# Two of four tiles' membership tests in an experts' routing: from VectorE alone to ScalarE and VectorE

## The chip, the cores and the metric

The kernel runs on one core of a Trainium2 chip. The metric is device time in microseconds (us), the median of several executions. A profiled execution of the kernel gives the trace that the numbers below come from.

## What is computed

Four layers run over an input of 4 batches of 1024 positions with 256 features each: a state space layer, a feed-forward layer, a linear attention layer and the same feed-forward layer again. The change touches the feed-forward layer, which adds an MLP and a product-key mixture of 512 tiny experts:

```
routing = einsum("tnd,tdk->tnk", (h @ W_q).reshape(2, n, 64), keys)   # two scores of 64 keys each
sx, sy = top 8 of each;  all_scores = sx[:, :, None] + sy[:, None, :]  # 64 pairs
scores, pk = top_k(all_scores, 8);  indices = 64 * ix + iy             # 8 experts of 512
ew = silu(x . down_embed[indices]) * softmax(scores)
out = mlp(x) + sum over the 8 of ew * up_embed[indices]
```

Keys of the first kind that can give an expert number below 512 are only the first 8 of 64; a larger number is taken as 511, the last expert.

## The kernel before

The 4096 positions are eight groups of 512, and a group is four tiles of 128 positions (the partitions). The kernel never gathers rows of the experts. For each position it makes a dense table `tb` of 512 weights, almost all of them zero, transposes it on TensorE (`st`), multiplies it into the dense activations `wt` of all experts, and sends that through `up_emb`.

`route` makes the table of one group. Its steps follow each other through small tiles: `r` holds the scores (copied from PSUM by ScalarE), `v` the top 8 values (MAX8 on VectorE), `d` exponentials, `code` a rank code of each of 64 second keys, and `most` a threshold for each of 8 first keys. `entries(m)` fills `tb` for tile `m` with 8 ScalarE activations of 64 elements. The last three operations, on VectorE, compare every code to every threshold (`eq`, 4 tiles x 8 x 64 = 2048 elements), multiply `tb` by this mask of 0 and 1, and add `last` to the last expert's column.

`route` is a Python generator, cut into steps by `yield`. It is used in two places.

In the **experts stage** (`experts`, line label L46 in the trace since a helper records every operation) all engines' queues stand in an order written by hand. A loop takes eight steps `k` per group. In each step it advances `apply` (the table's use for this group, with `emb` products on TensorE and `silu` on ScalarE), then `routes[g]`, then, at k = 5, 6 and 7, `routes[g + 1]` (scores, copy to `r`, top 8 to `v`), and at the end `beside`, which puts in parts of the state space layer's last groups and of their MLP (tiles `gate`, `tanh`, `up`, `av`, `down`, `xw`). The tiles of `route` have one buffer each here. The PSUM banks of `emb`, `gate`, `up`, `down` and others are three, taken in turn. At k = 0 of the next group the transposes `st` of tiles 0 and 1 read `tb`; those of tiles 2 and 3 wait until VectorE has multiplied the first two into `wt`.

In the **last FFN** (`ffn`) a scheduler orders each engine's queue. `route(0)` stands before the first group; `route(g + 1)` stands between `chosen(g)`, which uses the table of g, and `raise_x(g)`, a long run of TensorE products into the output. Each group has eight pairs of products `gate` and `up` into four PSUM banks; ScalarE takes the silu of the first into `s` (L1509), VectorE multiplies it by the second (`act`, L1511).

Of the kernel before, what the change touches and what calls it, by code (L numbers as in the profile page):

```python
# [13 lines left out]
AF = mybir.ActivationFunctionType  # L14
ALU = mybir.AluOpType
# [4 lines left out]
P = 128  # L20
# [4 lines left out]
NG = NT // G  # L25
# [3 lines left out]
NEXP, NKEY, TOPK, INTER = 512, 64, 8, 1024  # L29
# [21 lines left out]
class Net:  # L51
# [1064 lines left out]
    def route(self, nc, w, g, hT, pools, got, ps=None):  # L1116
# [8 lines left out]
        dve = nc.vector  # L1125
# [33 lines left out]
        def eights(name):  # L1159
            return sm.tile([P, M4, TOPK], F32, tag=name, name=name)  # L1160
# [28 lines left out]
        sht = [P, M4, TOPK, NKEY]  # L1189
        tb = tables.tile([P, M4, NEXP], F32, tag="tb", name="tb")  # L1190
        tbv = tb.rearrange("p m (i j) -> p m i j", i=TOPK)
# [20 lines left out]
        code = sm.tile([P, M4, NKEY], F32, tag="code", name="code")  # L1212
# [11 lines left out]
        for i in range(M4):  # L1224
# [5 lines left out]
        first, rank = r[:, 0:M4, 0:TOPK], eights("rank")  # L1230
# [14 lines left out]
        most, last8 = eights("most"), eights("last8")  # L1245
# [15 lines left out]
        eqv = eq.rearrange("p m j b -> p m (j b)").rearrange(  # L1261
            "p m (i j) -> p m i j", i=TOPK
        )
        dve.tensor_tensor(
            eqv, code.unsqueeze(2).to_broadcast(sht),
            most.unsqueeze(3).to_broadcast(sht), ALU.is_ge,
        )
        yield
        dve.tensor_tensor(tbv, tbv, eqv, ALU.mult)
        dve.tensor_tensor(tb[:, :, NEXP - 1], tb[:, :, NEXP - 1], last, ALU.add)  # L1270
        got.append(tb)

# [39 lines left out]
    def experts(self, w, xpool, xs, hs, rest):  # L1312


        tc, nc, ends, mlps, bank = self.tc, rest.engines, rest.ends, rest.mlps, rest.bank
        with ExitStack() as ctx:
# [16 lines left out]
            asks, hT, routes, tables = dict(rest.first_h), {}, {}, {}  # L1333
# [4 lines left out]
            def load(into, g):  # L1338
                while g == NG - 1 and ends.next_cost():
                    ends.stage()  # L1340
                tag = "hT" if into is hT else f"ask{g // half}"
                into[g] = two.tile([P, KD, G], F32, tag=tag, name=tag)
                nc.sync.dma_start(out=into[g], in_=hs[g])
# [7 lines left out]
            def begin(g):  # L1351
                tables[g] = []
                ps = None if g else rest.route0
                routes[g] = self.route(nc, w, g, asks, (one, one, one, rp), tables[g], ps)
                next(routes[g])
# [75 lines left out]
            def beside(cost):  # L1431
                left[0] = min(left[0] + 3.5, 6.0) - cost
                for q in (ends, mlps):
                    c = q.next_cost()
                    if c is not None and c[0] <= left[0]:
                        q.stage()
                        left[0] -= c[0]
# [7 lines left out]
            for step in range(8 * NG + 6):  # L1445
                g, k = step // 8, step % 8
                if k == 0 and g < NG:
                    while g not in rest.stored:
                        ends.stage()
                        mlps.stage()  # L1450
                    self.x[g] = xpool.tile([P, TG, D], F32, tag=f"x{g}", name=f"x{g}")
                    nc.sync.dma_start(out=self.x[g], in_=xs[g])
                if k == 2 and g < NG:
                    applied.append(apply(g))
                for a in list(applied):
                    if next(a, self) is self:
                        applied.remove(a)
                if g < NG:
                    next(routes[g], None)
                if g + 1 < NG:  # L1460
                    if k == 5:
                        begin(g + 1)
                    if k > 5:
                        next(routes[g + 1])

                    if k == 5 and g % 2 == 0 and g + 2 < NG:
                        load(asks, (g + 2) // 2)
                        load(asks, (g + 2) // 2 + half)
                    if k == 6:
                        load(hT, g + 1)  # L1470
                beside(COST[k])

    def ffn(self, w, out):
        nc, tc = self.nc, self.tc
        with ExitStack() as ctx:
# [18 lines left out]
            def route(g):  # L1494
# [3 lines left out]
                return got[0]  # L1498

            table = route(0)  # L1500
            for g in range(NG):
                h = hT[g]
                act = []
                for c in range(IC):
                    cs = slice(c * P, (c + 1) * P)
                    pg = self.product(mm, [(w["gate_w"][:, k, cs], h[:, k, :]) for k in range(KD)])
                    pu = self.product(mm, [(w["up_w"][:, k, cs], h[:, k, :]) for k in range(KD)])
                    s = two.tile([P, G], F32, tag="s", name="s")
                    nc.scalar.activation(s, pg, AF.Silu)  # L1509
                    a = acts.tile([P, G], F32, tag="act", name="act")  # L1510
                    nc.vector.tensor_tensor(a, s, pu, ALU.mult)  # L1511
                    act.append(a)
                wt = self.chosen(two, stp, mm, w, h, table)
                if g + 1 < NG:
                    table = route(g + 1)
                self.raise_x(op, g, w, wt, act)
                self.store(out, g)
# [71 lines left out]
```

## Time and profile before

| what | us |
|---|---|
| median of 3 runs | 2068.34 (2068.19 to 2068.84) |
| the profiled execution's own time | 2070.76 |
| its span, first to last instruction | 2069.0 |
| VectorE busy with `eq<-code,most`, 16 times | 36.6 |
| VectorE busy with `tb<-tb,eq`, 16 times | 36.6 |
| experts stage, from the first table to the last | about 1119 to 1357 of the span |
| last FFN | about 1588 to 2069 of the span |

The span is the profiled time without what lies around it. A row of busy time adds up the instructions of one form; it says how long they ran, not that the kernel would be shorter by as much without them.

### The profile page before, as it was taken

The page shows a single profiled execution, that of the slowest core. Times are in us where ns is not written, and L with a number is a line of the kernel's source. Part 1 is how long each engine was busy: PE and PEld are TensorE (multiplying, and loading weights), DVE is VectorE, ACT ScalarE, POOL GpSimd, SP SyncE. Part 2 cuts the span into 40 slices and gives each one's busy share as a digit, 9 for nine tenths or more (in the row PEclk, how much of TensorE's full clock was granted, in tenths as well). Part 3 has the DMA queues.
Part 4 walks back from the last instruction along what each step waited for, and adds up shares of the span by engine and source line. Part 5 has one row for each costly group of instructions (what it writes and reads, how often), then busy time and mean ns, then how long its engine had stood idle before and what let it go on. Part 6 is the DMA issues. An engine that isn't in the chain of part 4 may idle for free.

```text
span 2069.0 us, 22487 instructions
## 1 busy us (share of the span) xinstructions
PE 1806.8 (87%) x7402; PEld 1156.1 (56%) x7402; DVE 1643.7 (79%) x2845; ACT 1068.9 (52%) x2041; POOL 897.1 (43%) x607
## 2 busy tenths in 40 slices
PE   6777689888789898898868899889997999999999
PEld 2445445546456464564644656656765666556665
DVE  5799999999999999999999999954548644445551
ACT  3866667756777677677354454513333332333331
POOL 2978878888788887787751000011110000000000
PEclk9777899999999999999979999999998999999999
DMA  4111122221222212212123032120000000000000
GB/s 128 41 37 46 46 68 66 76 68 47 80 76 68 72 49 78 65 53 75 54 79 114 14 105 72 31 87 1 1 1 1 0 11 11 10 11 10 11 11 10
DMA packets 79926, 97.45 MB, mean 47 GB/s; under 512 B 7361, under 2 KB 53313, under 8 KB 79809
## 3 DMA queue, kind: packets, MB, share of 16 engines
q1 hardware_dynamic: 73232, 89.35, 14.3%
q10 hardware_dynamic: 6576, 6.67, 1.0%
q8 instruction: 58, 0.95, 0.2%
q14 instruction: 60, 0.48, 0.1%
HBM read 83.15 MB, written 12.85 MB: 46 GB/s over the span
## 4 chain that ended last, share of the span: by engine, by line
PE 44%; DVE 38%; issue 9%; ACT 7%; POOL 1%; DMA 0%; DVEq 0%; SPq 0%; ACTq 0%; POOLq 0%
PE ps L105 23%; DVE h L46 12%; DVE acc L46 10%; PE hT L46 2%; ACT a L46 2%; PE up L46 2%; PE dt L46 2%; PE gate L46 2%; DVE eq L46 1%; PE bc L46 1%; PE o L46 1%; PE out L46 1%; ACT xc L46 1%; PE xin L46 1%; PE tr L96 1%
## 5 line engine op out<-in xcount | busy, mean ns | idle before, releaser
L46 POOL TENSOR_TENSOR u<-dx,bt 128x1024 f32<-128x1024 f32 x255 | 602.6, 2364 | 199.2 <-DVE h L46 134.6
L46 PE MATMUL hT<-ident,h 128*128 128x128 f32 x2048 | 322.8, 299 | 147.4 <-DVE acc L46 145.7
L46 ACT ACTIVATE a<-delta,a_neg 128x512 f32<-128x512 f32 x512 | 342.4, 688 | 198.3 <-DVE h L46 197.1
L46 PEld LDWEIGHTS hT<-ident,h 128*128 128x128 f32 x2048 | 252.0, 152 | 291.1 <-DVE acc L46 251.4
L46 DVE SCALAR_TENSOR_TENSOR acc<-hT,cT,acc 128x512 f32<-128x512 f32 x512 | 354.9, 734 | 15.6 <-PE hT L46 15.2
L46 DVE TENSOR_TENSOR_SCAN h<-a,state,u 128x512 f32<-128x512 f32 x256 | 316.2, 1276 | 2.9 <-ACT a L46 1.6
L46 DVE TENSOR_TENSOR_SCAN h<-a,u 128x512 f32<-128x512 f32 x256 | 302.2, 1222 | 15.1 <-ACT a L46 15.0
L1511 DVE TENSOR_TENSOR act<-s,ps 128x512 f32<-128x512 f32 x64 | 44.0, 688 | 151.4 <-PE ps L105 151.3
L85 POOL TENSOR_TENSOR ri<-ri,mhalf 128x4 f32<-128x4 f32 x16 | 16.1, 1012 | 314.1 <-DVE ri L84 314.0
L46 PE MATMUL gate<-hT,gate_w 128*128 128x512 f32 x256 | 125.9, 615 | 8.8 <-ACT acc L46 8.8
L1509 ACT ACTIVATE s<-ps 128x512 f32<-128x512 f32 x64 | 38.1, 597 | 167.4 <-PE ps L105 164.6
L46 PE MATMUL up<-hT,up_w 128*128 128x512 f32 x256 | 121.9, 599 | 2.9 <-DVE xw L46 2.9
L105 PE MATMUL ps<-hT,w_gate_w 128*128 128x512 f32 x256 | 122.1, 600 | 2.5 <-DVE act L1511 2.5
L46 POOL TENSOR_TENSOR xc<-xc,tap 128x512 f32<-128x512 f32 x84 | 111.4, 1326 | 23.6 <-ACT tap L46 23.5
L46 PE MATMUL down<-w_down_w,av 128*128 128x256 f32 x512 | 119.7, 382 | 1.0 <-DVE xw L46 1.0
L105 PE MATMUL ps<-hT,w_up_w 128*128 128x512 f32 x256 | 120.4, 592 | 0.0
L105 PE MATMUL ps<-w_down_w,act 128*128 128x256 f32 x512 | 116.8, 380 | 3.0 <-DVE x L1308 3.0
L105 PEld LDWEIGHTS ps<-w_down_w,act 128*128 128x128 f32 x512 | 96.0, 190 | 21.6 <-DVE x L1308 8.8
L46 PEld LDWEIGHTS down<-w_down_w,av 128*128 128x128 f32 x512 | 96.1, 192 | 21.2 <-issue 8.6
L46 ACT ACT_TABLE_LOAD x63 | 80.8, 1283 | 29.5 <-DVE d L46 19.4
L1195 ACT ACTIVATE tb<-d,ex 128x64 f32<-128x64 f32 x256 | 62.0, 334 | 53.2 <-DVE ex L1185 53.2
L46 PE MATMUL out<-w_out_wT,y 128*128 128x256 f32 x256 | 70.1, 423 | 18.5 <-DVE y L46 18.3
(253 smaller groups left out, 3080.0 us busy)
## 6 DMA issues: line engine op xcount, KB each, us to landing
bt<-bcd SPq DMA_DIRECT2D x127, 256.0 KB, 3.3
gate_w<-in_gate_w SPq DMA_DIRECT2D x64, 128.0 KB, 2.5
up_w<-in_up_w SPq DMA_DIRECT2D x64, 128.0 KB, 2.2
in_wT<-in_in_wT SPq DMA_DIRECT2D x8, 512.0 KB, 3.8
hs<-hT SPq DMA_DIRECT2D x8, 512.0 KB, 3.0
xs<-xw SPq DMA_DIRECT2D x8, 512.0 KB, 2.7
hT<-hs SPq DMA_DIRECT2D x8, 512.0 KB, 4.3
x<-xs SPq DMA_DIRECT2D x8, 512.0 KB, 4.4
```

What stands on the lines that cost most here:

```text
L46: return self.tc.keep_in_program_order(f(*args, **kw))
L85: nc.gpsimd.tensor_tensor(ri, ri, self.mhalf.to_broadcast([P, TG]), ALU.pow)
L96: self.nc.tensor.transpose(ps[:, t * P : (t + 1) * P], src[:, t, k * P : (k + 1) * P], self.ident)
L105: self.nc.tensor.matmul(ps, lhsT=lhsT, rhs=rhs, start=i == 0, stop=i == len(pairs) - 1)
L1195: nc.scalar.activation(tbv[:, m, i, :], d[:, M4 + m, 0:NKEY], AF.Copy, scale=ex[:, m, i : i + 1],)
L1509: nc.scalar.activation(s, pg, AF.Silu)
L1511: nc.vector.tensor_tensor(a, s, pu, ALU.mult)
```

## The change

For tiles 2 and 3, ScalarE now makes the difference `most - code` (Identity with scale -1 and the threshold as a bias per partition), 8 activations of 64 elements for each tile, and VectorE takes "difference <= 0" and the multiplication by `tb` in one operation with three operands. For tiles 0 and 1 VectorE compares and multiplies as before, over 1024 elements instead of 2048. The generator has one more `yield`, before the fused operation, and in the experts stage step k = 7 advances `routes[g]` once more, after `routes[g + 1]`: the top-8 search of the next group stands before the fused operation.

```diff
+        first, others, shh = slice(0, 2), slice(2, 4), [P, 2, TOPK, NKEY]
+        for m in (2, 3):
+            for i in range(TOPK):
+                nc.scalar.activation(
+                    eqv[:, m, i, :], code[:, m, :], AF.Identity, scale=-1.0,
+                    bias=most[:, m, i : i + 1],
+                )
         dve.tensor_tensor(
-            eqv, code.unsqueeze(2).to_broadcast(sht),
-            most.unsqueeze(3).to_broadcast(sht), ALU.is_ge,
+            eqv[:, first], code[:, first].unsqueeze(2).to_broadcast(shh),
+            most[:, first].unsqueeze(3).to_broadcast(shh), ALU.is_ge,
         )
         yield
-        dve.tensor_tensor(tbv, tbv, eqv, ALU.mult)
+        dve.tensor_tensor(tbv[:, first], tbv[:, first], eqv[:, first], ALU.mult)
+        yield
+        dve.scalar_tensor_tensor(
+            tbv[:, others], eqv[:, others], 0.0, tbv[:, others], ALU.is_le, ALU.mult
+        )
         dve.tensor_tensor(tb[:, :, NEXP - 1], tb[:, :, NEXP - 1], last, ALU.add)
...
                     if k > 5:
                         next(routes[g + 1])
+                if k == 7 and g < NG:
+                    next(routes[g], None)
+                if g + 1 < NG:
 
                     if k == 5 and g % 2 == 0 and g + 2 < NG:
```

## The prediction

> **What bounds the kernel now.** I read the page first, then busy time by stage, then the waits of the stage, then the order of time around the changed lines, since only there can one see which wait ends last.
>
> ```profile
> PE 1806.8 (87%) x7402; PEld 1156.1 (56%) x7402; DVE 1643.7 (79%) x2845; ACT 1068.9 (52%) x2041; POOL 897.1 (43%) x607
> PE   6777689888789898898868899889997999999999
> DVE  5799999999999999999999999954548644445551
> ACT  3866667756777677677354454513333332333331
> ```
>
> The routing runs twice: in slices 22 to 26 (first experts stage) and from slice 31 on (last FFN). In the first VectorE is at 9; in the second TensorE is, and VectorE is half idle. Busy time by stage says it in us (columns: stretch, length, PE, PEld, DVE, ACT, POOL, clock, DMA share, GB/s):
>
> ```profile
> 1119.00:1357.00 238.00, 212.82 (x838) 143.77 (x837) 223.37 (x560) 116.24 (x331) 7.57 (x11) 0.94 0.20 65
> 1588.00:2069.00 481.00, 471.06 (x1645) 292.53 (x1643) 235.60 (x562) 149.44 (x384) 0.00 (x0) 0.99 0.03 9
> ```
>
> VectorE is busy 94% of the experts stage; in the last FFN it is 49%, and TensorE 98%. Who TensorE waits for in the experts stage (us in all, times, longest):
>
> ```profile
> PE st L46 <- DVE wt L46: 14.4, 6, 3.1
> PE st L46 <- DVE tb L46: 9.7, 3, 4.6
> ```
>
> Once a group TensorE stops for VectorE and then runs on almost without a gap until the next such stop. So a delay of VectorE moves everything behind it. In the last FFN the same delay costs nothing unless TensorE waits.
>
> **The change, instruction by instruction.** The groups by form (count | busy us, mean ns | idle before):
>
> ```profile
> L46 DVE TENSOR_TENSOR eq<-code,most 128x2048 f32<-128x2048 f32 x8 | 18.3, 2285 | 0.1
> L46 DVE TENSOR_TENSOR tb<-tb,eq 128x2048 f32<-128x2048 f32 x8 | 18.3, 2287 | 0.4
> L46 DVE SCALAR_TENSOR_TENSOR av<-up,av 128x512 f32<-128x512 f32 x12 | 8.2, 681 | 0.0
> L46 ACT ACTIVATE tb<-d,ex 128x64 f32<-128x64 f32 x256 | 63.0, 336 | 36.8 <-DVE ex L46 36.8
> ```
>
> VectorE loses two passes over 2048 elements (2.29 us each) for each of 16 routings, and gets three over 1024. No pass of 1024 is in the trace. Between the 512 (0.69, the tensor-tensor d<-r,v; 0.68 for the three-operand form above) and the 2048 the slope is 1.04 ns an element, so 1.22 us each, 3.67 instead of 4.58: 0.92 us saved a routing, 14.7 us in all, of which only the 7.3 of the experts stage lie on its path. Bounds for the new three-operand pass: 1.20 to 1.25 from the two 512 rows.
>
> ScalarE gets 16 activations of 64 elements a routing. Nearest row: tb<-d,ex, the same shape with one pointer operand (there scale, here bias). The experts stage in order of time, second routing (start, us, engine, line, operation; the brackets give idle time and who ended it):
>
> ```profile
> 1165.34 0.59 ACT L46 COPY r<-route 128x512 f32<-128x512 f32 x1 [1.19 <-PE route L46]
> ...
> 1166.19 0.42 DVE L46 TENSOR_REDUCE most<-pw 128x32 f32<-128x256 f32 x1
> 1166.65 2.29 DVE L46 TENSOR_TENSOR eq<-code,most 128x2048 f32<-128x2048 f32 x1
> ...
> 1169.19 2.29 DVE L46 TENSOR_TENSOR tb<-tb,eq 128x2048 f32<-128x2048 f32 x1
> ...
> 1171.51 0.17 DVE L46 TENSOR_TENSOR tb<-tb,last 128x4 f32<-128x4 f32 x1
> 1171.59 1.10 DVE L46 MAX8 v<-r 128x8 f32<-128x64 f32 x8
> ...
> 1187.18 3.92 ACT L46 ACTIVATE tb<-d,ex 128x64 f32<-128x64 f32 x16
> ```
>
> Sixteen such activations take 3.92 us (0.239 from start to start). Here a rule of the Trainium skill weighs against the change: "VectorE: DVE Perf Modes", section on the TRN2 errata, holds that the SBUF latency of VectorE and ScalarE is exposed between instructions, so many small tiles pay it each time, and wants 512 elements or more. Taken at its word, 16 times 0.336 is 5.4 us. The row shows overlap, 3.92, and I use that; the rule's figure is the upper end, 1.45 us more for each of nine places below, +13.
>
> **Where it lands: the experts stage.** The built order puts the sixteen activations on ScalarE after silu(1) and ahead of r<-route, the next group's scores. In the rows above r is copied at 1165.34, before "most" is ready at 1166.61. Now r waits behind the sixteen: they start 0.12 us after "most" (the delay of tb behind ex at 1304.62), r starts 3.82 later and takes 0.59. On VectorE the eight MAX8 of the next group now stand between the half multiply and the new fused pass, and they need r. Call the end of "most" M: MAX8 starts at M+4.56, the fused pass 1.02 later (eight starts, 0.127 apart), the small add of "last" 1.25 after that, the next instruction 0.08 later: M+6.91. That includes the fused pass itself, so VectorE idles about 2 us and then does what it did before. Against the time of that next instruction before:
>
> Routing 1: M 1132.62, 1139.53 against 1139.47, +0.06 (two av passes used to sit there and now fill the wait). Routing 2: M 1166.61, 1173.52 against 1172.61, +0.91. Routing 3: M 1199.06, 1205.97 against 1204.92, +1.05. Routing 5: M 1261.74, +0.65. Routing 6: M 1291.24, +0.85. Routing 7: M 1321.59, +0.73 (against 1327.77).
>
> Routing 4 (M 1230.90) is worse, because work of the MLP stands in between:
>
> ```profile
> 1231.41 2.28 DVE L46 TENSOR_TENSOR eq<-code,most 128x2048 f32<-128x2048 f32 x1
> ...
> 1232.10 0.60 ACT L46 ACTIVATE tanh<-gate 128x512 f32<-128x512 f32 x1 [1.19 <-PE gate L46]
> ...
> 1233.62 0.68 DVE L46 SCALAR_TENSOR_TENSOR av<-tanh,gate 128x512 f32<-128x512 f32 x1
> ```
>
> That tanh comes after r in ScalarE's order, so it ends at M+5.02 = 1235.95 instead of 1232.70; VectorE, done with its half compare at 1232.6, stands at av until then. Then av 0.60, half multiply 1.14, MAX8 1.02, fused and last 1.33: 1240.05 against 1237.63, +2.4. TensorE's emb(3) also waits for this av to free a PSUM bank, but it is back before the wt multiply, which VectorE reaches 2.4 us late anyway.
>
> Routing 8 has no next group: fused pass at 1353.19 after the sixteenth activation, last ends 1354.61; the fourth transpose of tile 0 needs it and goes at 1354.75 instead of 1354.37, +0.4.
>
> Sum 7.1 us. It passes on: behind each routing TensorE's second pair of transposes waits for VectorE's wt. silu(2) and silu(3) also slip by 2 to 4 us behind the sixteen; they free PSUM banks, and TensorE loses up to 1 us for them, inside the 1.1 to 3.1 us that it waits for wt. The extra generator step at k=7 issues no instruction of its own and moves no DMA; POOL and SP keep their order.
>
> **Where it lands: the last FFN.** For routings 2 to 8 the sixteen run between tb and the first silu of the next pair while TensorE does the up and down products; in the routing at 1765 they end at 1771.2, with the table load s ends at 1773.0, and VectorE needs it at 1773.05. Cover is 0.05 us for VectorE and over 3 for TensorE, whose bank is wanted at 1776.22. Cost 0. The saved VectorE time is worth nothing there. Routing 1 has no previous group's down products to hide behind:
>
> ```profile
> 1605.49 1.06 ACT L1509 ACTIVATE s<-ps 128x512 f32<-128x512 f32 x2
> ...
> 1606.15 1.95 PE L105 MATMUL ps<-hT,w_gate_w 128*128 128x512 f32 x4
> ```
>
> The gate matmul at 1606.15 takes the bank that the first s frees. Now s starts at 1605.49+3.82 = 1609.3 and ends 1609.9, so TensorE starts at 1610.0, 3.85 late. Six transposes of tb move up into this gap by the new order and give back 0.8: +3.1.
>
> **Sum**: 7.1 + 3.1 = +10.2 us. The profiled execution took 2070.76 us (span 2069.0 and 1.8 around it), the median of the runs is 2068.34; +10.2 makes 2081.0 for the first and 2078.5 for the median.
>
> **Rivals.** Faster: a bias pointer costs ScalarE nothing, and the sixteen run as pointer-free ones would. "ScalarE: Activation LUTs", section "What ACT_TABLE_LOAD costs", states 93 ns for each pointer operand; without it the start-to-start time would be about 0.146 by estimate, and r would be 1.4 us earlier. The waits then fall under the saving in all routings but the fourth: -4 in the experts stage, +1.7 in the FFN, in all about -2; the sign turns where the sixteen take under 2.8 us (1.1 us off nine places). To pass -4.1 (0.2%) the FFN loss must vanish too, and VectorE's 7.3 come through: 2061. Against it: delta<-z with a bias pointer alone takes 687 ns where a plain copy of its size takes 586. Chance 0.05.
>
> Absorbed: half the delay of VectorE disappears in places where it waits for TensorE anyway (x<-o, 6.9 us in the stage). +3, 2071. Against it: those matmuls follow the late transposes. Chance 0.08.
>
> Much slower: no overlap among the sixteen (+13), or a bank freed late by silu(2) stops TensorE outside its idle time, some 1 us in each routing. 2086 to 2092. Chance 0.10.
>
> That the change does not do what it says is excluded by the built order, where all sixteen stand in each of 16 routings.
>
> **Numbers.** The forecast keeps 0.77. Range 2071 to 2086: from the absorbed case to where the much slower one begins. A measurement of this kernel tells about 0.2% (4.1 us) from no change. Faster 0.05, same 0.08, slower 0.87.
>
> **What would show it.** Right: three DVE rows of about 1.22 us; sixteen eq<-code,most on ACT in about 3.9 us; DVE v<-r waiting for ACT r, about 2 us in six of the routings; DVE av waiting for ACT tanh once for over 3 us; TensorE 3 us idle near 1606 of the old time; no change in routings 2 to 8 of the last FFN. Wrong: MAX8 without a wait, activations at 0.15 or 0.33 us, the experts stage (238.0 us before) not longer by 5 to 9 us, or the last FFN by more than 5.

## The result, and the profile after

The changed kernel takes 2079.26 us (median of 5 runs, 2078.35 to 2080.61), the kernel before on the same chip 2068.19 (2067.20 to 2068.84): ratio 1.0056, 95% interval 1.0041 to 1.0070. That is 11.1 us slower; 10.2 were predicted. The profiled execution of the changed kernel took 2078.35 us (span 2076.6).

The page's first line and three rows of slices:

```profile
PE 1807.6 (87%) x7402; PEld 1154.6 (56%) x7402; DVE 1627.9 (78%) x2861; ACT 1128.6 (54%) x2297; POOL 896.4 (43%) x607
...
PE   6767779888789897898877989889997999999999
...
DVE  5899999999999999999999889945548544445551
ACT  3866667766677666776454556523333433434441
```

VectorE has 15.8 us less to do than before (1643.7) and ScalarE 59.7 more (1068.9), yet the kernel is longer. Busy time by stage (stretch, length, PE, PEld, DVE, ACT, POOL, clock, DMA share, GB/s) and the groups of the new instructions:

```profile
1119.00:1357.00 238.00, 207.78 (x828) 139.53 (x828) 212.05 (x564) 142.20 (x451) 7.56 (x11) 0.96 0.20 65
...
1588.00:2076.00 488.00, 475.92 (x1656) 295.10 (x1654) 228.59 (x576) 181.51 (x513) 0.00 (x0) 0.99 0.03 9
```

```profile
L46 ACT ACTIVATE eq<-code,most 128x64 f32<-128x64 f32 x128 | 31.4, 334 | 17.6 <-DVE most L46 17.6
...
L46 DVE TENSOR_TENSOR eq<-code,most 128x1024 f32<-128x1024 f32 x8 | 9.8, 1220 | 0.1
L46 DVE TENSOR_TENSOR tb<-tb,eq 128x1024 f32<-128x1024 f32 x8 | 9.7, 1218 | 0.3
L46 DVE SCALAR_TENSOR_TENSOR tb<-eq,tb 128x1024 f32<-128x1024 f32 x8 | 9.7, 1209 | 1.4 <-ACT eq L46 1.4
```

In the 238 us around the experts stage VectorE falls from 223.37 to 212.05 us of busy time. That is more than the change saves there, since beside the longer stage less of its surroundings fits into the stretch. Between the same two places of the program (M, the end of routing 1's last reduction into `most`, and the end of the eighth addition of `last`) VectorE is busy for 208.8 us before and 200.9 after, and idle for 12.6 and 24.8: 7.9 us of work saved, 12.2 us of idle time added. What the engines wait for is in the waits of the stage (total, times, longest):

```profile
PE st L46 <- DVE wt L46: 15.5, 7, 3.3
PE st L46 <- DVE tb L46: 10.9, 5, 3.4
DVE v L46 <- ACT r L46: 9.3, 6, 1.9
DVE x L46 <- PE o L46: 5.4, 5, 2.4
DVE av L46 <- ACT tanh L46: 3.7, 3, 3.2
```

The third and the last row are new in this size: v<-r did not wait before, and av<-tanh waited 0.4 us. Routing 2 in order of time (start, us, engine, line, operation) shows the cause:

```profile
1163.19 1.23 DVE L46 TENSOR_TENSOR eq<-code,most 128x1024 f32<-128x1024 f32 x1
...
1163.19 3.93 ACT L46 ACTIVATE eq<-code,most 128x64 f32<-128x64 f32 x16 [2.49 <-DVE most L46]
...
1167.03 0.56 ACT L46 COPY r<-route 128x512 f32<-128x512 f32 x1
...
1167.62 1.11 DVE L46 MAX8 v<-r 128x8 f32<-128x64 f32 x8 [1.74 <-ACT r L46]
1168.65 1.21 DVE L46 SCALAR_TENSOR_TENSOR tb<-eq,tb 128x1024 f32<-128x1024 f32 x1
```

The sixteen activations fill ScalarE for 3.9 us, r is copied behind them, and VectorE stops 1.74 us in front of MAX8. In the FFN's first routing TensorE (start, us, operation):

```profile
1607.34 1.89 PE L105 MATMUL ps<-w_down_w,act 128*128 128x256 f32 x8
1609.36 0.88 PE L1289 MATMUL st<-ident,tb 128*128 128x128 f32 x6
1612.85 3.68 PE L105 MATMUL ps<-hT,w_gate_w 128*128 128x512 f32 x4 [2.61 <-ACT s L1524]
1616.37 1.88 PE L105 MATMUL ps<-hT,w_up_w 128*128 128x512 f32 x4
```

The predicted stop is there, filled in part by the six transposes. What was not predicted is the gate behind it: 3.68 us, where it took 1.95 before.

Where the time went is best read from lengths of stages within each trace (from M of routing 1 to the end of the eighth "last"; from there to the start of the FFN's first copy r, which is the attention; from there to the end). They repeat to 0.1 us where nothing was changed, while a profile's start of the experts stage varies by over 3 us from one execution to the next:

| kernel | experts | attention | last FFN | median, us | ratio to before, 95% interval |
|---|---|---|---|---|---|
| before | 221.42 | 232.43 | 482.6 | 2068.19 | |
| changed | 225.74 | 234.43 | 487.25 | 2079.26 | 1.0041 to 1.0070 |
| FFN only | 221.42 | 232.47 | 487.05 | 2072.97 | 1.0011 to 1.0028 |
| experts only | 224.39 | 234.36 | 482.6 | 2075.09 | 1.0019 to 1.0042 |
| r first | 216.27 | 233.92 | 482.6 | 2064.67 | 0.9977 to 0.9990 |
| FFN without its first routing | 221.40 | 232.48 | 482.5 | 2067.82 | 0.9990 to 1.0006 |
| tanh first | 214.70 | 235.15 | 482.5 | 2063.52 | 0.9975 to 0.9988 |
| VectorE only | 224.45 | 232.72 | 482.5 | 2071.19 | 1.0008 to 1.0021 |
| one tile | 218.61 | 233.43 | 482.5 | 2065.35 | 0.9981 to 0.9994 |
| FFN, first routing one tile | 221.35 | 232.42 | 483.71 | 2069.07 | 0.9999 to 1.0015 |
| d first | 212.75 | 233.95 | 482.6 | 2062.29 | 0.9955 to 0.9980 |
| FFN with the stop filled | 221.40 | 232.43 | 485.53 | 2071.11 | 1.0009 to 1.0024 |

(Each ratio is against runs of the kernel before beside it: medians 2068.3 for FFN only, experts only, r first and FFN without its first routing, 2068.06 for tanh first, VectorE only and the two one-tile kernels, 2069.09 for "d first", 2067.3 for the last row.)

For the change itself: 4.3 + 2.0 + 4.65 = 11.0, the 11.1 of the medians. (The two spans differ by only 7.6 because this execution entered the experts stage 3.4 us earlier than the one before.)

### The profile page after: what moved, and what is told of

It is laid out like the page before. It is cut to its first block, busy times and chain, and to the rows that moved or that the text cites. A ratio compares the mean times of both kernels' runs of the same rounds, so it can differ in the third digit from the quotient of the medians.

```text
span 2076.6 us, 22751 instructions
## 1 busy us (share of the span) xinstructions
PE 1807.6 (87%) x7402; PEld 1154.6 (56%) x7402; DVE 1627.9 (78%) x2861; ACT 1128.6 (54%) x2297; POOL 896.4 (43%) x607
## 5 line engine op out<-in xcount | busy, mean ns | idle before, releaser
L46 PE MATMUL gate<-hT,gate_w 128*128 128x512 f32 x256 | 124.3, 608 | 10.9 <-ACT acc L46 10.4
```

Of the source, the lines that this page charges most:

```text
L46: return self.tc.keep_in_program_order(f(*args, **kw))
```

## The experiments

The theory: what stands behind the sixteen activations in ScalarE's order is late, and that alone makes the kernel slower; where nothing that is needed soon stands behind them, they are hidden. Rival A: the activations, or the three-operand pass, cost a fixed price in each routing. Rival B: the loss is mostly TensorE's clock, falling differently from run to run. Rivals C to E are named where they come in. In all of these kernels `route` has an argument, `style`, that chooses the form of its last operations, so that the experts stage and the last FFN can differ; only the lines that matter are shown.

**FFN only.** The experts stage gets the old operations (the default of `style`) and the old loop.

```diff
-                for _ in self.route(nc, w, g, hT, (one, two, sm, mm), got):
+                for _ in self.route(
+                    nc, w, g, hT, (one, two, sm, mm), got,
+                    style="NEW" if g else "NEW",
+                ):
```

> Change only in the last FFN; the experts stage has the old compare, multiply and loop. Theory (work that stands behind the sixteen activations in ScalarE's order is late; elsewhere they are hidden): only the first of the eight FFN routings loses, +3.1 us by the prediction's sum, +4.7 by the trace of the changed kernel, so 2071.3 to 2073. Rival A (each routing pays a fixed price for its sixteen activations or its three-operand pass, wherever it stands): half of the 11 us of the whole change, 2073.7, spread evenly over the eight routings in the trace. Rival B (the change's 11 us are mostly TensorE clock episodes that fall differently from run to run): anything between 2066 and 2080, with no stop of TensorE behind s.

Measured +4.7 us, of which 4.5 are in the FFN's length; TensorE's stop and the slow gate are those of the changed kernel to 0.2 us.

```profile
1605.17 0.88 PE L1297 MATMUL st<-ident,tb 128*128 128x128 f32 x6
1608.64 3.51 PE L105 MATMUL ps<-hT,w_gate_w 128*128 128x512 f32 x4 [2.60 <-ACT s L1532]
```

**Experts only.** The last FFN gets the old operations.

> Change only in the experts stage; the last FFN as before. Theory: +7.1 by the prediction's sum, +6.3 by the trace of the changed kernel (4.3 in the stage and 2.0 until the FFN): 2074.5 to 2075.3. Rival A (fixed price for each routing): 2073.7. The two lie close here; what they differ in is the trace: theory has v<-r waiting for r in six places and av for tanh in one. With the FFN-only kernel the two parts must add up to the 11.1 of the whole; rival B (clock episodes by chance) has no reason for them to add up.

Measured +6.8; with the part above 11.5, so the halves add up to the whole within the intervals, for which rival B has no reason. The waits of the stage are those of the changed kernel, to the tenth:

```profile
DVE v L46 <- ACT r L46: 9.3, 6, 1.9
...
DVE av L46 <- ACT tanh L46: 3.7, 3, 3.2
```

Its profiled execution (2073.43) was the shortest of its runs, so its row in the table adds up to less than the median's 6.8: two half-clock stretches of TensorE at the stage's start, which the changed kernel's trace has at 1141.9 and 1176.0, are missing in it. That much, 1.35 us, is left of rival B: with the same operations the interval from routing 2 to routing 3 (from M to M) is 31.65 us here and 32.95 in the changed kernel.

**FFN without its first routing.** `style="NEW" if g else "OLD"`.

> Change in the last FFN's routings 2 to 8 only; its first routing and the experts stage as before. Theory: the sixteen activations are hidden behind the up and down products of the group before, 0.0, 2068.2 (within 1 us). Rival A (fixed price for each routing, seven eighths of the FFN's part): +4 to +4.8, 2072 to 2073.

Measured 0.9998 of the time before, and the FFN's length is that of before to 0.1 us: seven routings with 112 added activations cost nothing. Rival A, at 4 us or more, falls for the FFN. The whole loss there is that of the first routing.

**r first.** The change in the experts stage, with one call moved (against the changed kernel):

```diff
+                if k == 6 and g + 1 < NG:
+                    next(routes[g + 1])
                 if g < NG:
                     next(routes[g], None)
                 if g + 1 < NG:
                     if k == 5:
                         begin(g + 1)
-                    if k > 5:
+                    if k == 7:
                         next(routes[g + 1])
```

> Experts stage with the change, but with the next group's copy r<-route put ahead of the sixteen activations on ScalarE (one line moved in step k = 6); the last FFN as before. Theory: v<-r no longer waits; VectorE's last waits only 0.5 us for the sixteenth activation, so the instruction behind it comes at about M+5.4 where it came at M+6.0 to M+6.3 before: -0.6 to -0.85 in six routings, but +2.0 in routing 4, where tanh still stands behind the sixteen, and +0.4 in routing 8. Sum about -1.7 against the kernel before: 2066.5, and some 8 us under the experts-only kernel. Rival A (the activations or the three-operand pass cost by themselves, whatever waits behind them): as the experts-only kernel, 2074 to 2075.

Measured 2064.67: 3.6 us faster than before and 10.4 under the experts-only kernel, with the same instructions in another order. Routing 2:

```profile
1162.89 0.58 ACT L46 COPY r<-route 128x512 f32<-128x512 f32 x1 [1.19 <-PE route L46]
...
1164.19 3.92 ACT L46 ACTIVATE eq<-code,most 128x64 f32<-128x64 f32 x16 [0.72 <-DVE most L46]
...
1166.81 1.10 DVE L46 MAX8 v<-r 128x8 f32<-128x64 f32 x8
1168.15 1.23 DVE L46 SCALAR_TENSOR_TENSOR tb<-eq,tb 128x1024 f32<-128x1024 f32 x1 [0.24 <-ACT eq L46]
```

MAX8 no longer waits, and the next instruction comes at M+5.33 to M+5.34 in routings 2, 3, 5, 6 and 7 (5.4 expected; M is the end of "most"), in routing 4 at M+8.56. Rival A falls in the experts stage too. The gain is larger than expected: the added local gains come to about 2.5 us (1.7 expected; routing 1 gives 1.1), but the stage is 5.15 shorter. The rest goes with TensorE's clock: at the places where the FFN-only trace, which entered the stage at the same time to 0.02 us, has half-clock stretches of 3.4 us at 1144.1, 1178.3 and 1209.0, this one has none. TensorE's stops there are 2.05, 1.83 and 1.60 us instead of 3.08, 2.49 and 2.42. By the other traces the stretches are worth about what is missing: one at the second place cost 1.3 us (changed against experts only), the one at the third about 1.5 (before against changed, below); this is an estimate, and it was not tested by an experiment in this stage. The length of a stop does not decide alone, since the one-tile kernel below keeps the three stretches with stops near 2.0; the last section shows what does.

**tanh first.** The sixteen are put behind the MLP's work of step k = 6 as well, by a `yield` on either side of them and one more advance at the end of the step:

```diff
                     if k == 6:
                         load(hT, g + 1)
                 beside(COST[k])
+                if k == 6 and g < NG:
+                    next(routes[g])
```

> As the kernel with r first, but the sixteen activations are also put behind the MLP's work of step k = 6, so that in routing 4 tanh stands ahead of them; the other routings keep their ScalarE order. Theory (queueing behind the sixteen): routing 4's next instruction comes at about M+7.1 instead of M+8.56, and only that changes: -1.4 us against the r-first kernel, about 2063.2. Rival A (the activations or the three-operand pass cost by themselves): no change against the r-first kernel, 2064.7.

Measured 2063.52, and the experts stage is 1.57 shorter than with r first. The attention behind it is 1.23 longer, so the gain of the whole is not shown by the medians: 4.5 us under its own runs of the kernel before against 3.6 with r first, and the intervals overlap. What the trace shows is the local effect. In routing 4 av no longer waits, and the next instruction stands at M+6.97:

```profile
1224.40 0.60 ACT L46 ACTIVATE tanh<-gate 128x512 f32<-128x512 f32 x1 [1.19 <-PE gate L46]
1224.89 3.91 ACT L46 ACTIVATE eq<-code,most 128x64 f32<-128x64 f32 x16
1225.03 0.69 DVE L46 SCALAR_TENSOR_TENSOR av<-tanh,gate 128x512 f32<-128x512 f32 x1
```

**VectorE only.** Is it the saved VectorE time that the r-first kernel gains, or the earlier place of MAX8? Here the sixteen activations are left out, and tiles 2 and 3 get a compare and a multiplication of their own on VectorE (against the changed kernel):

```diff
-        dve.scalar_tensor_tensor(
-            tbv[:, others], eqv[:, others], 0.0, tbv[:, others], ALU.is_le, ALU.mult
-        )
+        dve.tensor_tensor(
+            eqv[:, others], code[:, others].unsqueeze(2).to_broadcast(shh),
+            most[:, others].unsqueeze(3).to_broadcast(shh), ALU.is_ge,
+        )
+        dve.tensor_tensor(tbv[:, others], tbv[:, others], eqv[:, others], ALU.mult)
```

> Experts stage with the split and the new place of the next group's MAX8 (between the halves), but without ScalarE: VectorE compares and multiplies tiles 2 and 3 too, in two more passes of 1024 elements, and no activation is added; the last FFN as before. Theory (what the r-first kernel gains is the VectorE time that the three-operand pass saves): nothing is saved, two more passes cost some 0.3 us a routing, so +2 to +2.5 against the kernel before, 2070.5. Rival C (the gain comes from MAX8 standing earlier, and with it the next group's chain): faster than before, 2065 to 2067. Rival A (splitting costs by itself, and that is what made the changed kernel slow): +6.8, 2075.

Measured +3.1, of which 3.0 in the experts stage. Splitting costs: the next instructions come 2.0 us later in sum over the eight routings (0.3 us a routing was estimated from the passes), and between routings 5 and 6 a half-clock stretch at 1274.0 that the trace before lacks goes with 1.3 us more. An early MAX8 alone gains nothing; rival C falls. Without the saved pass there is no gain; how much of the r-first kernel's 5.15 us is the pass itself and how much the clock is the estimate given there.

**One tile.** The change's own order in the experts stage, r behind the activations, but eight of them (against the changed kernel):

```diff
-        first, others, shh = slice(0, 2), slice(2, 4), [P, 2, TOPK, NKEY]
-        for m in (2, 3):
+        first, others, shh = slice(0, 3), slice(3, 4), [P, 3, TOPK, NKEY]
+        for m in (3,):
```

> Experts stage with the change's own ScalarE order (r behind the activations), but for one tile instead of two: 8 activations, VectorE compares and multiplies three tiles; the last FFN as before. Theory (queueing): r is copied at about M+2.0 to M+2.6, before VectorE has done its three quarters (M+3.5), so v<-r waits no longer; the next instruction comes at about M+5.4; routing 4 loses about 0.8. Sum about -4, 2064. Rival A (a price for each activation): half of the +6.8 of the experts-only kernel, +3.4, 2071.7.

Measured 2065.35, 2.7 us faster than before, where a price for each activation gives 3.4 slower. r ends before VectorE is done with its three quarters:

```profile
1163.56 2.02 ACT L46 ACTIVATE eq<-code,most 128x64 f32<-128x64 f32 x8 [2.49 <-DVE most L46]
1165.49 0.56 ACT L46 COPY r<-route 128x512 f32<-128x512 f32 x1
1165.57 1.75 DVE L46 TENSOR_TENSOR tb<-tb,eq 128x1536 f32<-128x1536 f32 x1
1167.24 1.11 DVE L46 MAX8 v<-r 128x8 f32<-128x64 f32 x8
```

So half of the activations do not cost half of the loss: they change its sign. The gain is smaller than the 4 us expected, since the next instruction comes at M+5.79 in routing 5 and M+5.59 in routing 6, and the attention is 1.0 longer.

**FFN, first routing one tile.** As FFN only, but routing 1 sends one tile to ScalarE (`style="NEW" if g else "ONE"`).

> As the FFN-only kernel, but in the first FFN routing only one tile (8 activations) goes to ScalarE. Theory (the stop of 2.6 us behind s is followed by a gate matmul of 3.5 us instead of 1.9, and the short stop is not): s is 1.9 us late instead of 3.85, TensorE stops 0.7 us, the gate takes 1.9: +1.1, 2069.4. Rival D (the slow gate has nothing to do with the stop, or the loss goes with the number of activations): half of the +4.7, 2070.6, with a gate of 3.5 us in the trace.

The FFN is 1.13 us longer than before (1.1 expected). The median, 2069.07 against 2068.06, does not tell this from no change or from rival D's 2070.6 (interval of the ratio 0.9999 to 1.0015); the trace does, since rival D had a gate of 3.5 us. The stop is not quite where it was expected: it is 1.20 us, ahead of the transposes, and behind it the gate takes 1.88.

```profile
1603.96 0.87 PE L1315 MATMUL st<-ident,tb 128*128 128x128 f32 x6 [1.20 <-DVE tb L1303]
1604.67 1.88 PE L105 MATMUL ps<-hT,w_gate_w 128*128 128x512 f32 x4
```

**FFN with the stop filled.** This isolates the slow gate. Everything is as in the FFN-only kernel, but the six transposes that stand in the stop are made three times:

```diff
-            self.nc.tensor.transpose(st[:, c, :], tb[:, i, c * P : (c + 1) * P], self.ident)
+            for _ in range(times if i < 2 and c < 3 else 1):
+                self.nc.tensor.transpose(
+                    st[:, c, :], tb[:, i, c * P : (c + 1) * P], self.ident
+                )
```

> As the FFN-only kernel, but in the first FFN routing each of the six transposes of tb that stand in TensorE's stop is made three times (the same values written again), so that TensorE works for 1.45 us more of the wait for s. Theory (the gate matmul of 3.5 us is a half-clock stretch brought on by the stop of 2.6 us): s and the start of the gate stay where they were, the stop is 1.2 us, the gate takes 1.9, and the FFN from the first copy r to the end takes 485.4 us in the trace instead of 487.05; 2071.3. Rival D (the gate is slow for another reason): gate 3.5 us, 487.0, 2073.

```profile
1604.18 2.19 PE L1298 MATMUL st<-ident,tb 128*128 128x128 f32 x18
1607.67 1.99 PE L105 MATMUL ps<-hT,w_gate_w 128*128 128x512 f32 x4 [1.30 <-ACT s L1535]
```

With twelve more transposes the FFN is 1.5 us shorter (485.53), and the gate takes 1.99. By the medians, each against its own runs of the kernel before, it is +3.8 against +4.7: the same direction, but the intervals overlap, so the trace carries this result. Rival D falls. The granted clock (the third column from the end) of the stretch from the start of the gate, first in the changed kernel, then here:

```profile
1612.90:1616.30 3.40, 3.40 (x4) 1.42 (x5) 1.94 (x4) 0.38 (x1) 0.00 (x0) 0.50 0.00 0
```

```profile
1607.70:1611.10 3.40, 3.40 (x8) 1.60 (x9) 1.97 (x4) 1.00 (x2) 0.00 (x0) 1.00 0.00 0
```

What is left, 485.53 - 482.6 = 2.9 us, is what the wait for s costs without the slow gate.

**d first.** With tanh first VectorE still waits for the sixteenth activation. Two subtractions of the next group, which need nothing but r and v, are moved in front of the three-operand pass (one `yield` behind them, one more `next(routes[g + 1])` at k = 7, and one more `next(routes[0])` ahead of the loop).

> As the kernel with tanh first, and the next group's two subtractions into d are put ahead of the three-operand pass on VectorE (0.8 us of work that otherwise comes behind it). Theory (VectorE still idles 0.5 us a routing for the sixteenth activation, and work put there is free): six routings gain up to 0.5 us, -2 to -3 us against the tanh-first kernel, 2060.5 to 2061.5. Rival E (TensorE's transposes wait for tb, and tb now ends 0.3 us later, so the gain is taken back): 2063.5 to 2065.5.

Measured 2062.29 against 2069.09 on the same chip, ratio 0.9967, the fastest kernel of the study: 6.8 us under the kernel before and some 17 under the changed one. The expectation counted from the tanh-first kernel's 2063.52, which was measured beside 2068.06; with the kernel before 1.03 higher, as here, it is 2061.5 to 2062.5, and rival E's 2064.5 to 2066.5. Rival E falls, though against tanh first (4.5 us under the kernel before) the intervals overlap. In the traces the experts stage is 1.95 shorter than with tanh first, and the wait in front of the three-operand pass is gone:

```profile
1168.60 0.69 DVE L46 TENSOR_TENSOR d<-r,v 128x512 f32<-128x512 f32 x1
1169.21 0.22 DVE L46 TENSOR_TENSOR d<-v 128x64 f32<-128x64 f32 x1
1169.35 1.22 DVE L46 SCALAR_TENSOR_TENSOR tb<-eq,tb 128x1024 f32<-128x1024 f32 x1
```

## Why the prediction was right, point by point

**Prices: right.** The three passes of 1024 elements take 1.21 to 1.23 us (1.22 estimated), the sixteen activations 3.92 to 3.93 from first start to last end (3.92 was taken from the row, and not the 5.4 of no overlap). They start 0.03 to 0.04 us after "most" where that is what they wait for, not the 0.12 taken from another pair; so everything came 0.09 earlier than the working said.

**Local delays in the experts stage: right.** Predicted was M+6.91 for the next instruction; it is M+6.82 in routings 1, 2, 3, 5, 6 and 7. In routing 4 it is M+9.04, 2.31 late against 2.4. For routing 8 the eighth "last" ends 0.5 later after its M (0.4 predicted). Summed over the eight: 6.5 us against 7.1. MAX8 waited in six of the routings, 1.0 to 1.9 us each.

**"It passes on": the step that failed.** The stage grew by 4.3 us in the changed kernel, not by the 6.5 of its local delays. That also misses the growth of 5 to 9 us whose absence the prediction named as a sign of being wrong. From M to M, the delays of routings 4, 5 and 7 arrive whole; of routing 2's 0.8 us 0.5 arrive, of routing 6's 0.8 us 0.4. Most is lost behind routing 3: the interval to routing 4 is 0.5 us shorter instead of 0.95 longer, which is 1.5 of the 2.2 us that are missing. TensorE there, first before, then after:

```profile
1210.24 1.97 PE L46 MATMUL st<-ident,tb 128*128 128x128 f32 x8 [2.43 <-DVE wt L46]
1212.01 2.72 PE L46 MATMUL gate<-hT,gate_w 128*128 128x512 f32 x4
```

```profile
1208.27 1.25 PE L46 MATMUL st<-ident,tb 128*128 128x128 f32 x8 [2.60 <-DVE wt L46]
1209.36 1.88 PE L46 MATMUL gate<-hT,gate_w 128*128 128x512 f32 x4
```

Before, a half-clock stretch begins at 1210.3; after, none does, though the stop is no shorter. In the same interval VectorE's wait for o falls from 1.7 to 0.4 us (in the stage from 6.9 to 5.4). This is the wait of the absorbed rival, but TensorE, which it waits for, is also faster here, so it is not a second saving beside the clock.

**The attention: missing in the sum.** 2.0 us were lost behind the stage, in both kernels with the change's own order there. Two stretches of the trace before, where the second has its clock back, and the two of the trace after, with the clock at 0.50 for 6.8 us:

```profile
1353.60:1357.00 3.40, 3.02 (x13) 2.52 (x14) 1.78 (x4) 0.00 (x0) 0.00 (x0) 0.50 0.16 61
1357.00:1360.40 3.40, 3.40 (x19) 3.04 (x18) 2.13 (x4) 0.00 (x0) 0.00 (x0) 0.99 0.45 114
```

```profile
1353.50:1356.90 3.40, 1.90 (x8) 1.51 (x9) 2.62 (x4) 0.94 (x2) 0.00 (x0) 0.50 0.57 233
1356.90:1360.30 3.40, 3.40 (x13) 2.82 (x12) 1.53 (x3) 0.00 (x0) 0.00 (x0) 0.50 0.30 45
```

The o products behind it took 7.07 us and take 8.19 now. This accounts for some 1.1 of the 2.0; the remainder lies in the places of the later half-clock stretches at 1551 and 1575. It was not tested by an experiment, and the r-first, tanh-first and d-first kernels lose 1.5 to 2.7 us there too, so it is not the price of what waits behind the sixteen.

**The FFN: the mechanism right, its size off.** Seven routings at zero: right (482.5 against 482.6). Routing 1: s 3.82 us late behind the sixteen as predicted; the term +3.1 is 2.9 when the stop is filled. What the sum lacked is the gate at half clock, 1.5 to 1.7 us more. The trace before had the pattern 7 us ahead of the very place:

```profile
1599.19 3.63 PE L105 MATMUL ps<-hT,w_gate_w 128*128 128x512 f32 x4 [2.46 <-DVE act L1511]
```

A stop of 2.46 us, then a gate of 3.63 instead of 1.88. The working costed a stop at its own length and not at what follows it.

So the total was right to 0.9 us partly because its errors cancelled: 2.8 too much in the experts stage, 3.6 too little behind it. Of the rivals, "faster" came closest to what the change can do: it named the sign's turning point as sixteen activations under 2.8 us, and with eight in 2.0 us the sign did turn. Its own reason, a bias pointer that costs nothing, did not come true: the sixteen start 0.24 us apart, as in the working. Neither "no overlap" nor banks late by 1 us in each routing happened.

## What to carry to other kernels

Before work is moved to an idle engine, look at what stands behind it in that engine's order and who waits for that: here the same instructions gave +6.8 us or -3.6 depending on whether one copy of 0.6 us stood behind or in front of them. A busy share of 52% says that an engine has time, not that it has it at that moment. And a stop of the engine that sets the time is to be costed with what follows it: look in the trace for a like stop, and for the length of the same instruction behind it. That cost can differ between executions of the same operations, as the 1.3 us between routings 2 and 3 do.

## What the runs showed of the hardware

TensorE's granted clock is 1.00 or 0.50 in these traces, and from the experts stage on it is 0.50 in stretches of 3.4, 6.8, 10.2 or 13.7 us (but for the last of each trace, at its end). In the FFN every stop of 2.46 to 2.61 us before a gate was followed by one (gates of 3.3 to 3.7 us instead of 1.9), and stops of 1.20 and 1.30 us were not; in the experts stage a stop of 2.05 us was and one of 2.60 was not. The traces tell why. Within each of them all starts and ends of the stretches lie on one grid of 3.413 us, to 0.02 us, and what goes ahead of a stretch is a cell of this grid in which TensorE was busy for little of the time. From 1119 us on, in the twelve traces together, 86 cells at full clock were followed by half clock, and TensorE was busy for at most 0.42 of each; 3063 were not, and it was busy for at least 0.47 of each. (In the stages before, cells between 0.41 and 0.55 went either way.) So it matters how a stop lies across the grid:

| trace | stop of TensorE | cell of the grid | TensorE busy | clock of the next cell |
|---|---|---|---|---|
| changed | 2.05 us, 1138.66 to 1140.71 | 1138.5 to 1141.9 | 0.40 | 0.50 |
| changed | 2.60 us, 1205.67 to 1208.27 | 1203.3 to 1206.7 | 0.69 | 1.00 |
| | | 1206.7 to 1210.1 | 0.55 | 1.00 |
| FFN only | 2.60 us, to 1608.64 | 1604.9 to 1608.3 | 0.29 | 0.50 |
| stop filled | 1.30 us, to 1607.67 | 1604.0 to 1607.4 | 0.67 | 1.00 |

At the three places of the experts stage named under "r first" the cells were busy 0.37, 0.27 and 0.29 in the FFN-only trace (all followed by half clock), 0.40, 0.41 and 0.42 with one tile (all followed), and 0.71, 0.69 and 1.00 with r first (none followed; its third stop lies one cell earlier, busy 0.53). A stretch went on after cells busy up to 0.82 (and one of 0.88) and ended after 0.87 or more; in the attention above the first cell was busy 0.89 before, and 0.56 after. Busy shares are the profile's, in which the ends of matmuls are modelled. The rule is read from the traces; the filled stop is the one kernel that was made to change a cell, and its gate ran at full clock.

The Trainium skill ("TensorE: Matmul & The Clock Gate", section "Part 1: The HAM clock gate") has a free-running window of about 3.4 us behind this and puts the drop to half clock after at least one idle window of that length. The grid agrees; that the window must be idle does not: here cells in which TensorE was busy for up to 0.42 of the time were enough, and a stop of 2.05 us made one. Adding twelve transposes of some 0.1 us each to a stop of 2.60 us made the FFN 1.5 us shorter.
